# Places of routed tokens by quarters, rows scattered within the loop over groups, scaling on ScalarE

## The chip, the cores and the metric

One core of a Trainium2 chip runs the whole program. The metric is the device time of one execution in microseconds; the time before is the median of three runs.

## The reference, cut to what matters

The model has two blocks over 8192 tokens (32 sequences of 256) with 128 features. Each block computes `x + s * silu(g)`, where `s` comes from an attention branch and `g` from a feed-forward branch with experts, both fed with the normalised `x`. Block 0 has two transformer layers and 64 experts with a capacity. The change lies in block 1, whose routed part sends each token to one of 32 experts:

```python
shared_out = _swiglu(x, shared_gate_w, shared_up_w, shared_down_w)
logits = x @ gate_w
topk_ids = jnp.argmax(logits, axis=-1)
topk_val = jnp.max(logits, axis=-1)
scores = jax.nn.sigmoid(topk_val)[:, None]
xs = x * scores
tokens_per_expert = jnp.zeros((E,), jnp.int32).at[topk_ids].add(1)
order = jnp.argsort(topk_ids)
sorted_x = xs[order]
g = _grouped_mm(sorted_x, routed_gate_w, tokens_per_expert)
u = _grouped_mm(sorted_x, routed_up_w, tokens_per_expert)
d = _grouped_mm(jax.nn.silu(g) * u, routed_down_w, tokens_per_expert)
inv = jnp.argsort(order)
routed_out = d[inv]
return (shared_out + routed_out).reshape(b, s, h)
```

Its attention branch is a linear attention with 16 heads of 8 features, a product of two states per sequence, a norm over the features and an output product. Sequences don't depend on one another.

## The kernel before

The 64 tiles of 128 tokens are worked on in 16 groups of 4 tiles (`NG` = 16, `GT` = 4). Each piece of work is a Python generator that yields after a step; `run` takes a step of each of its generators in turn, and `rolling(steps, lag)` starts a new group every `lag` rounds. So the written order is an interleaving. A planner then orders each engine's queue anew, from dependencies, free buffers and its own estimates of time, and on the chip each queue runs strictly in order. NoSync edges given by hand bind that order on one engine without a wait.

Block 1 has these stages.

1. **The loop over groups** (`begun`, a `rolling` of `begin(g)` with lag 2). Its first steps lie beside the last units of block 0; `drain(begun)` runs the rest. For a group, `route(g)` loads the two parts of the block 0 experts' result (c_g, c_m, SyncE queue), adds them on GpSimd (POOL, L185), applies silu (ACT), multiplies and adds on VectorE (DVE), and normalises with `normed(..., act)`: statistics on DVE (L108, L109), small operations on POOL (L110 to L119), four activations on ACT (L121) into c_xn. Then come transposes on TensorE (PE, L131), router products (L205), maxima and indices on DVE (L213, L214), one-hot rows `hot`, the score, and the scaled rows `s_all` by four POOL operations (L224). Products with a triangle and with ones give each token's rank among those of its group with the same expert, and `before[:, g + 1]`, the counts of each expert up to this group (L232 to L240). `shared1(g)` computes the shared expert (L250 to L267).
2. **Places.** After the loop the counts of all groups are known. Each expert's share of the 96 pages (`S1` = 96 pages of 128 rows in the DRAM buffer `xslot`) is its count rounded up to 128. DVE computes where each expert's pages begin and from that `dest`, the place of each token (L811 to L839), and `widx`, the weight row of each page, with one small product on PE.
3. **Scatter beside linear attention.** `send()` issues one indirect DMA a tile from POOL's queue (L845, 64 in all; "sends" below), each of 128 rows of 129 numbers, the last being the token's number. After each send the written order has one step of `attending`, a `rolling` with lag 3 of `linear_attention(g)` for the first 15 groups. Such a group has ten steps and an end, 11 turns, and so 165 turns in all. Its norm (`normed(..., vec)`, eighth step) has three small operations on POOL (L110, L111, L113) between DVE's statistics and DVE's scaling; an order edge holds a later send behind the last norm written. The group's result goes to `s_all` (L929), the same memory that the sends read.
4. **Pages beside attention.** `routed()` takes pages in fours. It loads four pages from `xslot` (e_x, L938, after the last eight sends have landed), transposes them, and for each page loads the owner's weights (e_w, 384 KB, L958), multiplies (L961, L970) and scatters the result to `back` by an indirect DMA on POOL (L975). Four pages are five turns, 120 in all; a turn of attention and a turn of pages alternate, and what is left of the one runs alone.
5. **The end.** The sixteenth attention group runs beside `finish(g)`: load from `back`, two products with the identity that add the shared part (L996, L997), silu, multiply, add, store.

Work tiles are shared by tags ("gate", "tok", "chan", "out", "wide") in two pools, `works[0]` with one buffer a tag and `works[1]` with two; `work(n)` picks one of them by n % 3. In the loop "gate" holds c_g and "out" the shared expert's result.

Of the kernel before, what the change touches and what calls it, by code (L numbers as in the profile page):

```python
# [16 lines left out]
F32 = mybir.dt.float32  # L17
I32 = mybir.dt.int32
# [42 lines left out]
def recurrent_kernel(ctx: ExitStack, tc: tile.TileContext, x, consts, small0, wsd, wgu, wd, small1, bias1, wr, out):  # L61
# [87 lines left out]
    def room(pool_, gs):  # L149
        for g in gs:  # L150
            x_at[g] = pool_.tile([P, GT, D], F32, name=f"x_{g}")
            xt_at[g] = pool_.tile([P, GW], F32, name=f"xt_{g}")
            if g % 4 == 0:
                hots[g // 4] = pool_.tile([P, NT // 4, E1], F32, name=f"hot_{g // 4}")
# [4 lines left out]
    def begin1(pool_):  # L159
        t = at1["sw_c"] = pool_.tile([P, n_s1 - cut], F32, name="sw_c")  # L160
        sp.dma_start(t, small1[:, cut:])
        at1["rank"] = pool_.tile([P, NT], F32, name="rank")
        at1["before"] = pool_.tile([P, NG + 1, E1], F32, name="before")
        vec.memset(at1["before"][:, 0], 0.0)
        at1["ones"] = pool_.tile([P, P], F32, name="ones")
        vec.memset(at1["ones"], 1.0)
        at1["eiota"] = pool_.tile([P, E1], F32, name="eiota")
        pool.iota(at1["eiota"], [[1, E1]], base=0, channel_multiplier=0, allow_small_or_imprecise_dtypes=True)
        room(pool_, range(EARLY))
# [7 lines left out]
    def route(g):  # L177
# [20 lines left out]
        normed(wk, x_at[g], xn, act)  # L198
        yield
# [23 lines left out]
        for j in range(GT):  # L223
            pool.tensor_scalar(s_all[:, g * GT + j], xn[:, j], score[:, j : j + 1], 0.0, ALU.mult, ALU.add)  # L224
# [15 lines left out]
        vec.tensor_reduce(at1["rank"][:, tl], pos, AX.X, ALU.add)  # L240
        yield
# [53 lines left out]

    def begin(g):
        yield from route(g)
        yield from shared1(g)
# [499 lines left out]
    before, rank, ones = at1["before"], at1["rank"], at1["ones"]  # L798
# [3 lines left out]
    siota = w1p.tile([P, 1], F32, name="siota")  # L802
    pool.iota(siota, [[0, 1]], base=0, channel_multiplier=P, allow_small_or_imprecise_dtypes=True)

    drain(begun)


    dest = w1p.tile([P, NT], I32, name="dest")
    widx = w1p.tile([1, S1], I32, name="widx")
    pad = w1p.tile([P, E1], I32, name="pad")  # L810
    vec.tensor_scalar(pad, before[:, NG], float(P - 1), None, ALU.add)  # L811
    vec.tensor_scalar(pad, pad, 7, 7, ALU.logical_shift_right, ALU.logical_shift_left)
    padf = w1p.tile([P, E1], F32, name="padf")
    vec.tensor_copy(padf, pad)
    ends = w1p.tile([P, E1], F32, name="ends")
    vec.tensor_tensor_scan(ends, ones[:, :E1], padf, 0.0, ALU.mult, ALU.add)
    vec.tensor_tensor(padf, ends, padf, ALU.subtract)

    late = w1p.tile([S1, E1], F32, name="late")
    owner = w1p.tile([S1, 1], F32, name="owner")  # L820
    vec.tensor_scalar(late, ends[:S1], siota[:S1], None, ALU.is_le)
    vec.tensor_reduce(owner, late, AX.X, ALU.add)
    vec.tensor_scalar(owner, owner, float(E1 - 1), float(P), ALU.min, ALU.mult)
    diag = w1p.tile([S1, S1], F32, name="diag")
    vec.tensor_scalar(diag, ident[:S1, :S1], owner, None, ALU.mult)
    ps = bank()
    pe.matmul(ps[:1, :S1], ones[:S1, :1], diag, start=True, stop=True)
    vec.tensor_copy(widx, ps[:1, :S1])
    nq = 4
    for q in range(nq):  # L830
        tq = slice(q * NT // nq, (q + 1) * NT // nq)
        gq = slice(q * NG // nq, (q + 1) * NG // nq)
        vec.tensor_tensor(before[:, gq], before[:, gq], bcast(padf, 1, NG // nq), ALU.add)
        hq = hots[q].rearrange("p (g t) e -> p g t e", t=GT)
        for j in range(GT):
            vec.tensor_tensor(hq[:, :, j], hq[:, :, j], before[:, gq], ALU.mult)
        pos = w1p.tile([P, NT // nq], F32, name=f"pos{q}")
        vec.tensor_reduce(pos, hots[q], AX.X, ALU.add)
        vec.tensor_tensor(dest[:, tq], pos, rank[:, tq], ALU.add)  # L839

    sent, returned, last_norm = [], [], []

    def send():
        for t in range(NT):
            ins = pool.indirect_dma_start(  # L845
                out=xslot, out_offset=bass.IndirectOffsetOnAxis(ap=dest[:, t : t + 1], axis=0),
                in_=s_rows[:, t], in_offset=None,
            )

            if sent:  # L850
                tc.declare_no_dep(ins.ins, group="sent", reason="the rows are disjoint")
            tc.add_to_no_dep_group("sent", ins.ins)
            sent.append(ins)
            if last_norm:
                tc.add_manual_dep(ins.ins, last_norm[-1].ins.name, order, reason="norms go before")
            yield

    def linear_attention(g):
# [6 lines left out]
        q2 = work(g).tile([P, GT, D], F32, tag="gate", name="l_q2").rearrange("p t d -> p (t d)")  # L865
# [48 lines left out]
        o = work(g).tile([P, GT, D], F32, tag="tok", name="l_o")  # L914
# [7 lines left out]
        ot = work(g).tile([P, GW], F32, tag="chan", name="l_ot")  # L922
# [11 lines left out]
    def routed():  # L934

        for i in range(S1 // GT):
            xg = wk.tile([P, GT, D + 1], F32, name="e_x", bufs=2)
            ins = sp.dma_start(xg, rows(xslot, i))  # L938
            for d in sent[-8:]:
                tc.add_manual_dep(ins.ins, d.ins.name, waits, reason="reads what all the scatters wrote")  # L940
# [6 lines left out]
            xt = work(i).tile([P, GW], F32, tag="chan", name="e_xt")  # L947
            act.copy(xt, ps)  # L948
            ys = work(i).tile([P, GT, D], F32, tag="out", name="e_ys")
            yield  # L950
            for j in range(GT):
                wt = wk.tile([P, 3 * F1], F32, name="e_w", bufs=6)
                at = i * GT + j
                row = nc.values_load(
                    widx[:, at : at + 1], engines={mybir.EngineType.SP}, min_val=0, max_val=(E1 - 1) * P,
# [30 lines left out]
    def finish(g):  # L986

        tl = slice(g * GT, (g + 1) * GT)
        tag = ("gate", "tok", "chan", "out")[g % 4]
        gr = work(g // 4 + g).tile([P, GT, D], F32, tag=tag, name="f_g")  # L990
        ins = sp.dma_start(gr, rows(back, g))
        for d in returned[-8:]:
            tc.add_manual_dep(ins.ins, d.ins.name, waits, reason="reads what all the scatters wrote")

        ps = bank("sc", 4)
        pe.matmul(ps, ident, xt_at[g], start=True, stop=False)  # L996
        pe.matmul(ps, ident, gr.rearrange("p t d -> p (t d)"), start=False, stop=True)  # L997
        act.activation(gr, ps.rearrange("p (t d) -> p t d", d=D), AF.Silu)
        yield
        vec.tensor_tensor(gr, gr, s_all[:, tl], ALU.mult)  # L1000
        vec.tensor_tensor(gr, gr, x_at[g], ALU.add)
        sp.dma_start(rows(out, g), gr)
        yield

    sending, routing = send(), routed()
    attending = rolling([linear_attention(g) for g in range(NG - 1)], 3)
    while len(sent) < NT:
        next(sending, None)
        next(attending, None)
# [92 lines left out]
```

## Time and profile before

| | |
|---|---|
| median of 3 runs | 1380.33 us (1379.74 to 1383.29) |
| the profiled execution's own time | 1386.77 us |
| its span, from the first to the last instruction | 1384.8 us |
| mean granted TensorE clock | 0.958 |
| busy: PE, DVE, ACT, POOL | 1244.0, 956.0, 775.8, 684.9 us |
| last ranks of the loop (L240) | 959.6 us |
| first and last send (L845) | 963.7 and 1074.5 us |
| last page scatter (L975) | 1341.3 us |

The page of the profile gives busy time by engine, the span in slices, the DMA queues, the chain of work that ended last, and groups of instructions with their mean time and the idle time before them. A table by stage gives, for each stretch of time, each engine's busy time with the number of instructions in brackets, the granted clock, the share of time in which the DMA engines were busy, and GB/s. A timeline row has the start, the time taken, engine, line, operation, what is written and read, how many, and in square brackets how long the engine sat idle before it and what ended that.

### The profile page before, as it was taken

To read this page: it belongs to the slowest core of one execution; us is meant where nothing else is said; L and a number is where in the kernel's file an instruction comes from. 1 tells how busy PE (TensorE), PEld (TensorE's weight loads), DVE (VectorE), ACT (ScalarE), POOL (GpSimd) and SP (SyncE) were. 2 spreads that over 40 slices of the span, in tenths; PEclk is the share of its full clock that TensorE was granted. 3 is DMA by queue.
4 is the path that set the end of the run, shared out by engine and by line. 5 is a ranking of instruction groups with operands and counts; after the bars stand their busy time and mean duration, and the time that the engine had idled before them with its cause. 6 is when DMAs were issued, how large, how long until landed. Compare 5 with 4: busy or idle time off the path is not lost.

```text
span 1384.8 us, 22930 instructions
## 1 busy us (share of the span) xinstructions
PE 1244.0 (90%) x7425; PEld 877.7 (63%) x7425; DVE 956.0 (69%) x3091; ACT 775.8 (56%) x1842; POOL 684.9 (49%) x1052
## 2 busy tenths in 40 slices
PE   6988999899989999999997989899766889999898
PEld 4645665656655776667764666566454778788763
DVE  4689898968965566765655878777755665666437
ACT  1775566576746767667675566453533545545343
POOL 6254428272246766676646354442566344343440
PEclk9999999999989999999998999999977899999999
DMA  6021323310221221122201142512311557666667
GB/s 187 11 54 54 103 85 96 109 42 11 92 82 27 54 52 45 28 39 54 52 7 35 47 122 69 142 32 68 110 49 52 166 158 217 194 195 202 182 196 204
DMA packets 141927, 128.95 MB, mean 93 GB/s; under 512 B 17808, under 2 KB 117104, under 8 KB 141680
## 3 DMA queue, kind: packets, MB, share of 16 engines
q1 hardware_dynamic: 130032, 111.72, 27.5%
q0 software_dynamic: 11776, 15.78, 5.1%
q8 instruction: 59, 0.97, 0.3%
q14 instruction: 60, 0.49, 0.1%
HBM read 85.20 MB, written 42.25 MB: 92 GB/s over the span
## 4 chain that ended last, share of the span: by engine, by line
PE 56%; DVE 18%; ACT 8%; POOL 6%; issue 6%; DMA 4%; another core or an unknown queue 1%; SPq 0%; POOLq 0%; ACTq 0%; DVEq 0%
PE ps_mm L673 6%; PE ps_mm L655 6%; PE ps_sc L578 4%; PE ps_mm L619 3%; PE ps_tr L131 3%; PE ps_tr L610 3%; PE ps_mm L550 3%; PE ps_sc L961 3%; PE ps_sc L880 3%; PE ps_mm L970 3%; DMA e_x<-xslot 2%; PE ps_tr L902 2%; PE ps_mm L560 2%; PE ps_mm L633 2%; POOL bn_rs L111 2%
## 5 line engine op out<-in xcount | busy, mean ns | idle before, releaser
L975 POOL DMA_INDIRECT back<-e_ys,e_toi x96 | 97.0, 1011 | 139.0 <-ACT e_ys L974 112.9
L593 ACT ACTIVATE a_pr<-ps_sc,a_nm 128x256 f32<-128x256 f32 x256 | 119.2, 478 | 68.1 <-DVE a_nm L584 68.1
L110 POOL TENSOR_SCALAR bn_rs<-bn_mv 128x4 f32<-128x4 f32 x112 | 26.0, 232 | 229.2 <-DVE bn_mv L109 214.0
L655 PE MATMUL ps_mm<-xt,sw 128*128 128x512 f32 x256 | 134.3, 629 | 3.8 <-ACT r_ex L390 2.0
L124 POOL TENSOR_SCALAR z<-s_rows,bn_rs 128x128 f32<-128x128 f32 x256 | 129.4, 517 | 6.9
L673 PE MATMUL ps_mm<-sw,m_h 128*128 128x128 f32 x1024 | 127.3, 279 | 2.1 <-ACT a_at L625 1.1
L673 PEld LDWEIGHTS ps_mm<-sw,m_h 128*128 128x128 f32 x1024 | 119.6, 193 | 14.0 <-issue 5.3
L660 DVE SCALAR_TENSOR_TENSOR m_h<-m_h,m_z 128x512 f32<-128x512 f32 x128 | 89.7, 707 | 46.4 <-ACT m_h L659 45.3
L516 POOL DMA_INDIRECT moe<-e_y,sidx x64 | 93.0, 1453 | 57.8 <-ACT e_y L512 41.6
L111 POOL TENSOR_TENSOR bn_rs<-bn_rs,power 128x4 f32<-128x4 f32 x112 | 115.1, 1028 | 1.3
L657 ACT ACTIVATE m_z<-ps_mm,fold 128x512 f32<-128x512 f32 x128 | 86.8, 687 | 36.4 <-PE ps_mm L655 36.1
L584 DVE TENSOR_REDUCE a_nm<-ps_sc 128x2 f32<-128x512 f32 x128 | 83.1, 681 | 34.4 <-PE ps_sc L578 30.6
L961 PE MATMUL ps_sc<-e_xt,e_w 128*128 128x128 f32 x768 | 101.5, 279 | 3.0 <-ACT e_xt L948 2.2
L961 PEld LDWEIGHTS ps_sc<-e_xt,e_w 128*128 128x128 f32 x768 | 94.6, 195 | 10.0 <-issue 5.9
L578 PE MATMUL ps_sc<-a_qk,a_qk 64*128 64x256 f32 x512 | 96.8, 417 | 0.5 <-ACT a_pr L593 0.3
L610 PE MATMUL ps_tr<-con,a_pr 128*128 128x128 f32 x512 | 76.9, 284 | 9.8 <-ACT a_pt L611 6.0
L610 PEld LDWEIGHTS ps_tr<-con,a_pr 128*128 128x128 f32 x512 | 59.7, 146 | 40.9 <-issue 21.2
L659 ACT ACTIVATE m_h<-m_z 128x512 f32<-128x512 f32 x128 | 80.1, 635 | 1.4
L619 PE MATMUL ps_mm<-a_pt,a_v 128*64 128x256 f32 x512 | 73.3, 406 | 5.6 <-ACT e_y L512 2.8
L845 POOL DMA_INDIRECT xslot<-s_rows,dest x64 | 65.1, 1018 | 24.3 <-issue 18.5
L611 ACT COPY a_pt<-ps_tr 128x512 f32<-128x512 f32 x128 | 70.6, 590 | 10.0 <-PE ps_tr L610 8.7
L970 PE MATMUL ps_mm<-e_w,e_hs 128*128 128x128 f32 x384 | 61.7, 288 | 13.9 <-DVE e_hs L967 9.6
(234 smaller groups left out, 2985.7 us busy)
## 6 DMA issues: line engine op xcount, KB each, us to landing
e_w<-in_wr_dram SPq DMA_DIRECT2D x96, 384.0 KB
xslot<-zero SPq DMA_DIRECT2D x4, 1548.0 KB
e_x<-xslot SPq DMA_DIRECT2D x24, 258.0 KB
e_wg<-in_wgu_dram SPq DMA_DIRECT2D x16, 384.0 KB
x_in<-in_x_dram SPq DMA_DIRECT2D x16, 256.0 KB
tab<-s_rows SPq DMA_DIRECT2D x16, 256.0 KB
moe<-s_y SPq DMA_DIRECT2D x16, 256.0 KB
moe<-zero SPq DMA_DIRECT2D x4, 1024.0 KB
```

What stands on the lines that cost most here:

```text
L111: pool.tensor_tensor(rs[:, 0], rs[:, 0], power, ALU.pow)
L124: ins = pool.tensor_scalar(dst[:, j], src[:, j], rs[:, 1, j : j + 1], rs[:, 0, j : j + 1], ALU.add, ALU.mult)
L516: pool.indirect_dma_start(out=moe0[e % 2], out_offset=bass.IndirectOffsetOnAxis(ap=sidx[:, 4 * q + e : 4 * q + e + 1], axis=0), in_=ye[:, ...
L578: pe.matmul(sc[h][:, j * SEQ : (j + 1) * SEQ], qk[0][hd, q0 : q0 + P], qk[1][hd, b * SEQ : (b + 1) * SEQ], start=True, stop=True,)
L593: act.activation(pr[:, n], sc[h][:, j * SEQ : (j + 1) * SEQ], AF.Exp, bias=nm[:, n : n + 1], accum_out=su[:, n : n + 1],)
L610: pe.transpose(pts[:, n * P : (n + 1) * P], pr[:, n, k * P : (k + 1) * P], ident)
L619: pe.matmul(av[h * DPH : (h + 1) * DPH, :SEQ], v[:, 2 * b + k, h * DPH : (h + 1) * DPH], pt[:, k, h], start=k == 0, stop=k == 1,)
L655: pe.matmul(ps, par("w1", l * FF0 + f * P, P), xt, start=True, stop=True)
L673: pe.matmul(ps[:, j * D : (j + 1) * D], hs[f][:, j * P : (j + 1) * P], par("w2", l * FF0 + f * D, D), start=f == 0, stop=f == 3,)
L961: pe.matmul(ps[:, c * P : (c + 1) * P], wt[:, c * P : (c + 1) * P], xt[:, j * P : (j + 1) * P], start=True, stop=True,)
L970: pe.matmul(yp[:, :D], hs[:, c * P : (c + 1) * P], wt[:, 2 * F1 + c * D : 2 * F1 + (c + 1) * D], start=c == 0, stop=c == 1,)
L975: ins = pool.indirect_dma_start(out=back, out_offset=bass.IndirectOffsetOnAxis(ap=toi[:, j : j + 1], axis=0), in_=ys[:, j], in_offset=None,)
```

## The change

Expert places are handed out by pages, a quarter of the tokens at a time. After every fourth group, `place(q)` looks at the counts so far, rounds them up to pages, and gives each expert the pages that it newly needs behind those given out before. An expert's pages are then no longer consecutive. A token's place is its rank, plus the rows given before, plus a jump where it falls into a new page. `place(3)` also sums the owners of the pages and makes `widx`.

The sends stand within the loop: behind the norm of group g, up to four sends whose quarter was placed (group 7 and later), which gives 36 sends within the loop and 28 after it. `keep_in_program_order` holds each send behind the POOL instruction written before it. The rows are scaled by four activations on ACT instead of four operations on POOL. The page loads wait for all sends, e_w has five buffers instead of six, and attention and pages use fixed pools for their tiles. The places' tiles use the tags "out" and "gate" of `works[1]`.

```diff
         xn = wk.tile([P, GT, D], F32, tag="tok", name="c_xn")
         normed(wk, x_at[g], xn, act)
+        for _ in range(4):
+            if len(sent) < NT and g >= len(sent) // (NT // 4) * 4 + 7:
+                next(sending)
         yield
...
         for j in range(GT):
-            pool.tensor_scalar(s_all[:, g * GT + j], xn[:, j], score[:, j : j + 1], 0.0, ALU.mult, ALU.add)
+            act.activation(s_all[:, g * GT + j], xn[:, j], AF.Copy, scale=score[:, j : j + 1])
...
+    def place(q):
+        wk = works[-1]
+        full, off, ends, before = at1["full"], at1["off"], at1["ends"][:, q], at1["before"]
+        tq, gq = slice(q * NT // 4, (q + 1) * NT // 4), slice(q * NG // 4, (q + 1) * NG // 4)
+        pad = wk.tile([P, E1], I32, name="p_pad")
+        vec.tensor_scalar(pad, before[:, (q + 1) * NG // 4], float(P - 1), None, ALU.add)
+        vec.tensor_scalar(pad, pad, 7, 7, ALU.logical_shift_right, ALU.logical_shift_left)
+        vec.tensor_copy(full[:, q + 1], pad)
+        new = wk.tile([P, E1], F32, name="p_new")
+        vec.tensor_tensor(new, full[:, q + 1], full[:, q], ALU.subtract)
+        last = at1["ends"][:, q - 1, E1 - 1 : E1] if q else 0.0
+        vec.tensor_tensor_scan(ends, at1["ones"][:, :E1], new, last, ALU.mult, ALU.add)
+        w = wk.tile([P, GT, NG // 4, E1], F32, tag="out", name="p_w")
+        jump = wk.tile([P, E1], F32, name="p_jump")
+        vec.tensor_tensor(jump, ends, full[:, q + 1], ALU.subtract)
+        vec.tensor_tensor(jump, jump, off[:, q], ALU.subtract)
+        vec.tensor_tensor(w[:, 0], bcast(full[:, q], 1, NG // 4), before[:, gq], ALU.subtract)
+        vec.tensor_tensor(w[:, 1], bcast(off[:, q], 1, NG // 4), before[:, gq], ALU.add)
+        vec.tensor_copy(w[:, 2], bcast(jump, 1, NG // 4))
+        vec.scalar_tensor_tensor(new, new, 0.0, jump, ALU.is_gt, ALU.mult)
+        vec.tensor_tensor(off[:, q + 1], off[:, q], new, ALU.add)
+        yield
+        hq = hots[q].rearrange("p (g t) e -> p g t e", t=GT)
+        got = wk.tile([P, 3, NT // 4], F32, name="p_got")
+        for n in range(3):
+            sel = wk.tile([P, NT // 4, E1], F32, tag="gate", name="p_sel")
+            vec.tensor_tensor(sel.rearrange("p (g t) e -> p g t e", t=GT), hq, bcast(w[:, n], 2, GT), ALU.mult)
+            vec.tensor_reduce(got[:, n], sel, AX.X, ALU.add)
+            yield
+        rank = at1["rank"][:, tq]
+        vec.tensor_tensor(got[:, 0], rank, got[:, 0], ALU.is_ge)
+        vec.tensor_tensor(got[:, 0], got[:, 0], got[:, 2], ALU.mult)
+        vec.tensor_tensor(got[:, 1], got[:, 1], rank, ALU.add)
+        vec.tensor_tensor(at1["dest"][:, tq], got[:, 0], got[:, 1], ALU.add)
+        placed.add(q)
+        yield
...
     def begin(g):
         yield from route(g)
+        if g % 4 == 3:
+            yield from place(g // 4)
         yield from shared1(g)
...
     def send():
         for t in range(NT):
...
             sent.append(ins)
-            if last_norm:
-                tc.add_manual_dep(ins.ins, last_norm[-1].ins.name, order, reason="norms go before")
+            tc.keep_in_program_order(ins)
             yield
...
-            for d in sent[-8:]:
+            for d in sent:
...
-                wt = wk.tile([P, 3 * F1], F32, name="e_w", bufs=6)
+                wt = wk.tile([P, 3 * F1], F32, name="e_w", bufs=5)
...
-        q2 = work(g).tile([P, GT, D], F32, tag="gate", name="l_q2").rearrange("p t d -> p (t d)")
+        q2 = works[0].tile([P, GT, D], F32, tag="gate", name="l_q2").rearrange("p t d -> p (t d)")
```

The old block of places after the loop (L808 to L839) is gone. Likewise the tiles of attention l_o and l_ot lie in `works[1]` and `works[0]`, and those of the pages e_xt and e_ys in `works[1]`. The page results' loads in `finish` wait for all scatters instead of the last eight. The written order after the loop is as it was: a send and a step of attention in turn until all 64 sends are written, then pages beside attention.

## Prediction

> **What bounds the kernel now.** I read the page first (PE busy 90% of the span, POOL 49%), then a table by stage of the part that the change touches: loop over groups to 963 us, rows scattered 963 to 1076, first page of the experts at 1090, pages beside attention to 1298, pages alone to 1342, end.
>
> ```profile
> core 0: us, PE busy (x) PEld busy (x) DVE busy (x) ACT busy (x) POOL busy (x), PEclk, DMA share, GB/s
> 963.00:1013.00 50.00, 35.61 (x138) 20.60 (x137) 35.85 (x102) 22.37 (x25) 31.20 (x34) 0.86 0.35 110
> 1013.00:1076.00 63.00, 44.98 (x192) 33.49 (x192) 37.59 (x99) 24.16 (x26) 41.08 (x46) 0.76 0.16 51
> 1090.00:1298.00 208.00, 191.19 (x1386) 165.39 (x1385) 126.76 (x371) 106.00 (x225) 87.47 (x99) 0.98 0.66 196
> 845.00:963.00 118.00, 109.77 (x608) 78.68 (x607) 87.18 (x407) 52.84 (x115) 41.41 (x89) 0.97 0.24 67
> ```
>
> While rows are scattered no engine is full: PE is busy 81 of 113 us, at a clock of 0.76 to 0.86. In the loop before it and among the pages after it PE is busy 92 to 93%. So the scatter stage is the loose one. POOL's timeline tells why.
>
> ```profile
> 979.00 0.96 POOL L845 DMA_INDIRECT xslot<-s_rows,dest  x1 [0.30 <-issue]
> 980.27 0.97 POOL L845 DMA_INDIRECT xslot<-s_rows,dest  x1 [0.30 <-issue]
> 991.02 0.19 POOL L110 TENSOR_SCALAR bn_rs<-bn_mv 128x4 f32<-128x4 f32 x1 [9.79 <-DVE bn_mv L109]
> 992.77 1.05 POOL L845 DMA_INDIRECT xslot<-s_rows,dest  x1 [0.17 <-issue]
> ...
> 1006.53 0.20 POOL L110 TENSOR_SCALAR bn_rs<-bn_mv 128x4 f32<-128x4 f32 x1
> ...
> 1012.36 0.98 POOL L845 DMA_INDIRECT xslot<-s_rows,dest  x1 [0.30 <-issue]
> ...
> 1074.47 0.95 POOL L845 DMA_INDIRECT xslot<-s_rows,dest  x1 [0.30 <-issue]
> ```
>
> Sends follow one another every 1.27 us (979.00, 980.27), but each stretch of 11 to 13 ends in an attention group's norm, for which POOL waits: five such waits, 27 us in the list of waits. So 64 sends tied to five norms last 963.7 to 1075.4, where 64 x 1.27 would be 81. The 28th send starts at 1012.36, after the second norm. Until the last has landed no page can start; the chain of waits shows it:
>
> ```profile
> 1074.47 2.36 DMA xslot<-s_rows,dest
> 1076.98 2.97 DMA e_x<-xslot
> ```
>
> What a page and an attention group cost beside each other comes from two counts by stage: page scatters (L975), then stores of finished attention groups (L929).
>
> ```profile
> 1102.00:1298.00 196.00, 69.42 (x69) 0.98 0.65 193
> 1311.00:1342.00 31.00, 16.02 (x18) 1.00 0.64 203
> ...
> 1102.00:1298.00 196.00, 5.49 (x9) 0.98 0.65 193
> ```
>
> Pages alone: 18 starts, 17 intervals, from 1310.1 to 1341.3, 1.84 us each. The nine stores run from 1102.4 to 1298.0, eight intervals: 24.5 us a group, in which the written order has 8.8 pages (11 attention steps, 5 page steps to 4 pages). Those pages alone would take 16.2, so beside pages **a group costs 8.3 us more**. Its PE time there (busy by count for L862, L870, L880, L902, L913, L131, L927) is 11.0. In the scatter stage groups came at 997.1, 1021.5, 1036.6, 1055.9 and 1074.1: **19.3 us each**.
>
> **The change, part by part.**
>
> *Sends in the loop.* Four at each of the groups 7 to 14 and 15 make 36; 28 stay behind the loop, one to an attention step. The 13th and 24th attention step hold the first two norms, and sends stay behind norms as before. Of the 28, the first 12 need places of the third quarter only and may go before the loop ends; the rest need the last quarter's places, some 7 us after its ranks, and the two norms. Those norms came at 991 and 1006.5, so the last send starts near 1012.4 instead of 1074.5: **-62.1 us**, with landing and first page after it unchanged (the last send started 15.2 us before the first page's scatter at 1089.7).
>
> *Attention that this leaves for later.* 64 steps lay beside the sends, 28 do now; 36 steps (3.3 groups) move. Of 165 steps 137 remain against 120 page steps, where 101 remained. So 19 steps move to where pages ran alone: 19/11 x 8.3 = **+14.3**. The other 17 have no pages beside them and come with the end stage, whose last group and 16 final products keep PE busy 35.8 of 43 us. I take PE time, 17/11 x 11.0 = **+17.0**, as the final products can fill gaps; ends 12.8 (8.3 a group) and 30 (19.3).
>
> *Places by quarters on DVE.* By rows of this trace a `place` is: pad .173 + .172, cast .182, scan .225, six 128x32 operations at .19, three 128x128 at .277 (L833), three times a 128x512 product at .695 (L194) with its sum at .667 (L838), four 128x16 at .156, three for the owner at .55: 7.8 us, 7.2 of it before the places are there. Three lie in the loop, 23.4; the fourth (8.6 with its diagonal) replaces 10.8 after it. From 840 to 963 DVE is busy 91.4 of 123 us; 23.4 more is 93%, and PE is at 93% too. With 31.6 idle the cost lies between 0 and 23.4. DVE's queue is in order: behind a place stand the maxima and one-hot rows that PE's rank products wait for, and a place can itself wait, as its work tiles use the slots of c_g and f_y.
>
> *Sends on POOL in the loop.* The scaling takes 19.9 us off POOL (48 instructions, 845 to 963); 36 sends at 1.27 bring 45.7, so 67 of 118 us. Each quarter's first send waits for DVE's places; behind it stand the next group's sum (L185) and norm (L110 to L119), for which ACT's c_xn and then PE wait. The last norm is done at 919.2, its c_xn runs at 935.9: 17 us of cover. Gone, three waits of 7.2 us would cost up to 22. I take **+10** for DVE and POOL together, nearer to the idle time; ends 0 and 45.
>
> The sends here run beside a DVE that is busy 65% and take 954 / 958 / 2108 ns (least, median, most), so I keep 1.27 us. [...]
>
> *Scaling on ScalarE.* Four 128x128 activations take 1.65 us (L121), 26 us in all; ACT is busy 57 of 123 us and this is hidden. Without that cover it is 1.65 us a group. It ends ACT's waits for POOL's read of c_xn (10.8 us, six times), but PE hardly waited on those: nothing.
>
> *At nothing:* e_w with five slots instead of six (the list of waits has no wait for e_w between 1075 and 1345; cover is five pages at 2.8 us, and if it failed perhaps 5 us); waiting for all sends instead of the last eight (one queue, the last lands last); pages in another order (96 pages and as many weight loads); fixed slots for attention and pages.
>
> **Sum:** -62.1 + 14.3 + 17.0 + 10 = -20.8 us. The profiled execution took 1386.8 us, 2 more than its span of 1384.8, and 6.4 more than the median of 1380.3. So about 1366 for a profiled execution and **1360** for the median.
>
> **Rivals.**
>
> 1. *The loop grows by more than it saves (slower).* Place: the loop from group 7 on, where DVE and POOL are given 23 and 26 us net, and POOL stands at a send until DVE has the places. Price up to 45; from 31 on nothing is gained, and 41 gives 1390. For it: DVE at 83% from 880 to 900, PE at 96% in the last 43 us. Against: 31.6 us idle on DVE, POOL 40 us ahead of PE.
> 2. *The unpaired attention is paid at the scatter stage's price.* 17 steps at 19.3 a group are 30 instead of 17, with 15 in the loop: -3 to -8, so 1372 to 1377. For it: a lone group is a chain over five engines. Against: 16 final products are there to fill it.
> 3. *The moved attention is nearly free.* All 36 steps at 8.3 a group, 27, and a loop that doesn't grow: -35, 1345.
> 4. *The rows don't leave early.* If sends end up behind the norms of later groups, all 64 stay late, and the added DVE work is paid: 1385 to 1400.
>
> **How the numbers follow.** Main course 0.55, rival 1 0.18, rival 2 0.12, rival 3 0.10, rival 4 0.05. A difference within 0.3% (4 us) can't be told from none here. Faster: 0.52 + 0.08 + 0.10 = 0.70; same: 0.02 + 0.02 + 0.04 + 0.02 = 0.10; slower: 0.01 + 0.16 + 0.03 = 0.20. The main course alone is 1349 to 1375 (17 steps from 15 to 20, loop from 2 to 22). The range reaches over rivals 2 and 3 and half of rival 1: 1342 to 1390.
>
> **What would show it.** Right: 36 sends before the loop's last ranks, 28 after or around its end; about 50 us from the loop's end to the last send with two norms among them; first page scatter near 1038; mixed pages still near 2.8 us; attention stores after the last page scatter, and an end stage near 58 us instead of 43. Wrong: last ranks later than about 990 (rival 1); POOL waiting on dest for long before a send with PE idle; mixed pages above 3.0 us; an end stage over 75 us (rival 2).

## The result, and the profile after

The changed kernel took 1398.85 us (median of 4 runs, 1397.09 to 1400.21), the kernel before beside it 1381.81 us (4 runs): a ratio of 1.0133, with a 95% interval of 1.0103 to 1.0163. The forecast was 1360, faster. The profiled execution took 1397.09 us over a span of 1395.3.

By stages, in us (before, after, difference; predicted difference):

| stage | before | after | difference | predicted |
|---|---|---|---|---|
| last ranks of the loop | 959.6 | 999.2 | +39.6 | +10 |
| from there to the last send | 114.9 | 54.0 | -60.9 | -62.1 |
| from there to the first page scatter | 15.2 | 13.9 | -1.3 | 0 |
| page scatters, first to last | 251.7 | 267.7 | +16.0 | +14.3 |
| end | 43.5 | 60.5 | +17.0 | +17.0 |

All terms but one came out within 2 us. The loop's did not: it grew by more than is saved, which is what rival 1 forecast. ("Last ranks" is L253 in the changed kernel; a send is L371, a sum of c_g and c_m L195.) The table by stage of the changed kernel, whose stretches are the loop, the sends behind it, the pages and the end:

```profile
core 0: us, PE busy (x) PEld busy (x) DVE busy (x) ACT busy (x) POOL busy (x), PEclk, DMA share, GB/s
845.00:999.00 154.00, 106.84 (x512) 74.49 (x511) 89.91 (x433) 57.79 (x144) 73.84 (x93) 0.84 0.26 76
999.00:1053.00 54.00, 40.26 (x179) 24.86 (x177) 37.62 (x106) 25.34 (x31) 17.28 (x21) 0.91 0.30 89
1067.00:1335.00 268.00, 249.46 (x1790) 213.40 (x1790) 164.89 (x480) 140.01 (x296) 113.93 (x129) 0.99 0.61 188
1335.00:1395.00 60.00, 48.63 (x186) 25.96 (x184) 46.00 (x103) 23.35 (x31) 5.34 (x10) 0.98 0.53 150
```

In the loop PE is busy about as long as before (109.8 us then, 106.8 now) in 30% more time, and no engine is full: PE 69%, DVE 58%, POOL 48%. So the loop didn't get an engine that is busy all the time; it got waits. Its list of waits, 845 to 1003:

```profile
POOL c_g L195 <- DMA c_g<-moe: 33.0, 2, 20.7
ACT c_xn L121 <- POOL bn_rs L119: 31.6, 6, 12.5
...
POOL bn_rs L110 <- DVE bn_mv L109: 24.9, 4, 12.2
PE ps_tr L131 <- ACT c_xn L121: 22.2, 7, 7.8
...
DVE before L250 <- remote: 10.7, 1, 10.7
```

PE waits for c_xn, ACT for the norm on POOL, and POOL for DVE's statistics. (Before, ACT waited for L119 only 5.8 us between 860 and 964.) "Remote" stands where the profile knows no instruction that ended the wait. POOL's timeline shows what stands around a norm:

```profile
915.01 0.98 POOL L371 DMA_INDIRECT xslot<-s_rows,dest  x1 [3.45 <-ACT c_g L203]
916.82 0.96 POOL L371 DMA_INDIRECT xslot<-s_rows,dest  x1 [0.82 <-issue]
...
919.35 0.96 POOL L371 DMA_INDIRECT xslot<-s_rows,dest  x1 [0.30 <-issue]
920.39 0.19 POOL L110 TENSOR_SCALAR bn_rs<-bn_mv 128x4 f32<-128x4 f32 x1
920.66 0.22 POOL L117 TENSOR_SCALAR bn_rs<-bn_mv 128x4 f32<-128x4 f32 x1
921.03 1.02 POOL L371 DMA_INDIRECT xslot<-s_rows,dest  x1 [0.15 <-issue]
922.07 1.18 POOL L111 TENSOR_TENSOR bn_rs<-bn_rs,power 128x4 f32<-128x4 f32 x1
923.45 1.04 POOL L371 DMA_INDIRECT xslot<-s_rows,dest  x1 [0.20 <-issue]
924.52 0.21 POOL L119 TENSOR_TENSOR bn_rs<-bn_rs 128x4 f32<-128x4 f32 x1
```

Four sends stand ahead of the norm and two between its four operations. The plainest case is earlier: from 854.0 to 867.0 seven sends and a norm with two more sends in it pass through POOL, and from 861.5 on PE, DVE and ACT are idle together, for 5.5 us; they start again when the norm ends (ACT has waited 12.5 us for L119 then). From group 10 on the norms come at 907.6, 924.5, 935, 942, 947 and 966 us; before they came at 895, 898, 904, 908, 916 and 919.

### The profile page after: what moved, and what is told of

It reads as the page before. It is cut to its first block, busy times and chain, and to the rows that moved or that the text cites. A ratio compares the mean times of both kernels' runs of the same rounds, so it can differ in the third digit from the quotient of the medians.

```text
span 1395.3 us, 22978 instructions
## 1 busy us (share of the span) xinstructions
PE 1239.2 (89%) x7425; PEld 872.4 (63%) x7425; DVE 969.0 (69%) x3159; ACT 795.1 (57%) x1906; POOL 657.6 (47%) x988
## 5 line engine op out<-in xcount | busy, mean ns | idle before, releaser
L751 DVE SCALAR_TENSOR_TENSOR m_h<-m_h,m_z 128x512 f32<-128x512 f32 x128 | 89.7, 706 | 43.1 <-ACT m_h L750 42.3
L996 PEld LDWEIGHTS ps_sc<-e_xt,e_w 128*128 128x128 f32 x768 | 95.6, 195 | 14.4 <-issue 8.3
L371 POOL DMA_INDIRECT xslot<-s_rows,dest x64 | 63.8, 997 | 43.5 <-issue 36.5
L1009 ACT COPY e_ys<-ps_mm 128x128 f32<-128x128 f32 x96 | 25.4, 265 | 87.4 <-PE ps_mm L1005 78.2
## 6 DMA issues: line engine op xcount, KB each, us to landing
e_x<-xslot SPq DMA_DIRECT2D x24, 258.0 KB
```

Source lines behind the costliest of these rows:

```text
L751: vec.scalar_tensor_tensor(h, h, 1.0, z, ALU.add, ALU.mult)
L996: pe.matmul(ps[:, c * P : (c + 1) * P], wt[:, c * P : (c + 1) * P], xt[:, j * P : (j + 1) * P], start=True, stop=True,)
```

## The experiments

Kernels with the same chip in the table ran beside the kernel before on it. Chip I gave the result above; whether it is one of the later ones isn't known. Ratios are of medians, while the stages come from one profiled execution of each kernel. For most kernels that execution lies within 5 us of the median; those of e8 (1369.8 us, median 1362.3) and e10 (1390.9, median 1383.5) lie 7 us above, the slowest of theirs.

| kernel | chip (before there) | ratio, 95% interval | last ranks | last send, later by | pages | end |
|---|---|---|---|---|---|---|
| before | I (1381.8) | 1 | 959.6 | 114.9 | 251.7 | 43.5 |
| changed | I | 1.0133 [1.0103, 1.0163] | 999.2 | 54.0 | 267.7 | 60.5 |
| e1 sends written after the loop | II (1371.7) | 1.0112 [1.0073, 1.0151] | 988.8 | 89.2 | 243.3 | 43.2 |
| e2 sends two groups later | II | 1.0147 [1.0086, 1.0208] | 993.1 | 61.5 | 267.9 | 50.3 |
| e4 before, scaling on ACT | II | 0.9943 [0.9912, 0.9975] | 952.3 | 104.2 | 248.5 | 43.1 |
| e5 changed, scaling on POOL | II | 1.0040 [1.0015, 1.0065] | 989.2 | 45.0 | 261.5 | 61.8 |
| e8 norms before sends | II | 0.9934 [0.9909, 0.9959] | 986.9 | 45.7 | 260.7 | 60.8 |
| e10 own slots | II | 1.0081 [1.0054, 1.0108] | 1006.4 | 44.5 | 262.4 | 61.9 |
| e9 own slots, norms first | II | 0.9912 [0.9885, 0.9939] | 973.8 | 44.4 | 261.7 | 61.9 |
| e7 own slots, sends after loop | II | 1.0154 [1.0117, 1.0191] | 962.8 | 120.4 | 243.5 | 43.0 |
| e11 e9, statistics before places | III (1370.4) | 0.9875 [0.9821, 0.9929] | 973.5 | 44.8 | 266.1 | 52.3 |
| e13 e9, scaling on POOL | III | 0.9952 [0.9927, 0.9976] | 980.2 | 45.1 | 261.3 | 61.0 |
| e14 shared slots, sends after loop | III | 1.0124 [1.0055, 1.0193] | 963.8 | 113.5 | 246.4 | 43.1 |
| e12 e9, attention in the tail | IV (1371.6) | 1.0010 [0.9981, 1.0038] | 987.3 | 66.4 | 258.0 | 43.3 |
| e15 changed | V (1369.6) | 1.0018 [0.9998, 1.0037] | 986.8 | 46.0 | 259.0 | 61.9 |
| e16 before | V | 1.0012 [0.9993, 1.0031] | 960.8 | 105.8 | 245.1 | 43.5 |
| e17 e4 with filler | V | 1.0009 [0.9994, 1.0025] | 956.2 | 108.2 | 243.7 | 43.0 |
| e18 e9, two sends a step | V | 1.0027 [0.9999, 1.0055] | 963.9 | 73.1 | 269.0 | 43.1 |
| e19 changed | VI (1382.9) | 1.0116 [1.0078, 1.0154] | 1004.9 | 54.9 | 265.8 | 60.6 |
| e20 norms before sends (as e8) | VI | 1.0082 [1.0054, 1.0110] | 999.0 | 54.8 | 265.8 | 61.8 |

### First: which part of the change

e1 and e2 change the condition in `route`, e4 and e5 one line each:

```diff
 e1  -        for _ in range(4):
     +        for _ in range(0):
 e2  -            if len(sent) < NT and g >= len(sent) // (NT // 4) * 4 + 7:
     +            if len(sent) < NT and g >= len(sent) // (NT // 4) * 4 + 9:
 e4, in the kernel before:
     -            pool.tensor_scalar(s_all[:, g * GT + j], xn[:, j], score[:, j : j + 1], 0.0, ALU.mult, ALU.add)
     +            act.activation(s_all[:, g * GT + j], xn[:, j], AF.Copy, scale=score[:, j : j + 1])
 e5, in the changed kernel: the same line the other way
```

> The places stay in the loop and the scaling on ScalarE; only the 36 sends are taken out of the loop, so all 64 follow it, one to an attention step. Theory A (sends in POOL's queue hold up the norms of the loop's groups): the last ranks come back from 999 us to 960 to 970, the sends take about 111 us again, and the time is near the kernel before, 1380 to 1392. Theory B (the places' work on VectorE and their tiles in the slots of the loop stretch it): the last ranks stay near 990 to 1000 and the time is 1410 to 1425. Theory C (the scaling in ScalarE's queue stretches it): as B.

> As the changed kernel, but the first sends of a quarter stand behind the norm of the sixth group after its last (g >= 9, 13) instead of the fourth; 28 sends lie in the loop and 36 behind it. Theory A1 (POOL stands at sends whose places are not there yet): the waits before the 17th and 33rd send are gone, the last ranks come at 965 to 980, and the time is 1370 to 1385. Theory A2 (the sends' own 1.27 us between one norm and the next cost the time): last ranks 985 to 1000, time 1390 to 1402. Theory B (places) and C (scaling): last ranks near 999, time 1398 to 1406, as eight more sends follow the loop.

> The kernel before with one edit: the rows are scaled by four ScalarE activations a group instead of four POOL operations. Theory C (the scaling in ScalarE's queue stretches the loop): last ranks 970 to 1000 instead of 959.6, time 1390 to 1420. Theories A and B: last ranks within 5 us of 959.6 and the time within 5 us of the kernel before.

> The changed kernel with the scaling back on POOL, four operations of about 0.4 us a group. Theory C: the last ranks come earlier than 999 us, at 960 to 985, and the time falls to 1360 to 1385. Theory A: POOL has 1.5 us more a group in a queue that already holds up the loop, so last ranks 999 to 1015 and time 1398 to 1412. Theory B: no difference beyond 5 us.

e1 and e2 didn't do what they were made for. The planner moves a send to where its place is ready, wherever it was written: 44 and 47 sends still went before the last ranks (48 in the changed kernel), the first of them at 847.9 and 852.8 us. They tell nothing on the sends. e4 settles the scaling in the kernel before, and theory C fell: on ScalarE the last ranks come at 952.3, against 959.6 and 960.8 in the two profiles of the kernel before, and the median falls by 8.2 us. POOL is free of 44 operations, between 860 and 960 us alone, that stood among sums and norms. e5's time (1377 us) lies in theory C's range and its last ranks (989.2) in none; beside the changed kernel on chip V (e15, below) they are 2.4 us later, so there the scaling's place shows little.

### Second: sends, slots and places apart

To hold the sends, e7, e8 and e9 tie each by an order edge to a POOL operation of a norm (e7: that of the last group, with `range(0)` as in e1). e7, e9 and e10 give places tiles of their own.

```diff
+            scaled.append(pool.tensor_tensor(rs[:, 1], rs[:, 1], rs[:, 0], ALU.mult))
...
+            tc.add_manual_dep(ins.ins, scaled[-1].ins.name, order, reason="norms go before")
             tc.keep_in_program_order(ins)
... own slots:
-        w = wk.tile([P, GT, NG // 4, E1], F32, tag="out", name="p_w")
+        w = wk.tile([P, 2, NG // 4, E1], F32, name="p_w", bufs=1)
...
-            sel = wk.tile([P, NT // 4, E1], F32, tag="gate", name="p_sel")
...
+            for h in range(2):
+                sel = wk.tile([P, NT // 8, E1], F32, name="p_sel", bufs=1)
```

> The changed kernel, with every send ordered on GpSimd behind the norm that is written before it (the four of a step behind that group's own norm). The slots of the tiles of places stay those of the gate loads. Theory Q (sends stand in front of norms in GpSimd's queue, and that is the loop's growth): the last rank falls from 999.2 to about 965-970 us, the program to 0.985-0.99 of the kernel before. Theory S (the tiles of places take the slots that the gate loads of the last groups need, so the planner runs group 14 after group 15 and its load lands late): the last rank stays at 990-1000 and the ratio at 1.005-1.015. Theory D (VectorE's time for places in the loop): likewise 990 or more.

> The changed kernel, with tiles of their own for the places (the 2 KB tile of weights cut to its two parts that differ by group, the selection made in two halves of 1 KB, one buffer each), so that no gate load waits for a step of places; the sends are free to float as in the changed kernel. Theory S: groups run in order again, the last rank falls to about 965-970 us and the program to 0.985-0.99 of the kernel before. Theory Q: the sends still stand in front of norms, last rank 985-1000, ratio 1.005-1.015. Theory D: 990 or more, for VectorE's work is the same or slightly more (6 instructions more a quarter).

> Both edits together: tiles of their own for the places, and every send behind the norm written before it. Theories Q and S: last rank about 955-965 us, the last send 45-60 us later, ratio 0.975-0.985, whichever of the two is the cause (each alone then tells which). Theory D: the same work on VectorE, last rank still 985 or more and the ratio 1.00 or more.

> Tiles of their own for the places, and all 64 sends ordered behind the last group's norm: the places stay in the loop, no send does. Theory Q: last rank 950-960 us as with the scaling alone (952.3), the last send about 85-100 us later, ratio 0.99-1.00. Theory S: the same. Theory D: last rank 980 or more, since the places alone make the growth; ratio 1.01 or more.

Theory D fell as a whole: with places in the loop and every send behind its last norm (e7; 11 sends still start before the last ranks) the last ranks come at 962.8, 10.5 us after e4's. Places have a price, and it is the +10 that was meant for places and sends together. e9 adds the sends, norms first: 973.8, another 11.0, and 9 us later than either theory expected. e8 is e9 with shared slots: 986.9, another 13.1 by the profiles; but e8's is its slowest execution, and by the medians, on the same chip, it is 3.3 us (1362.3 against 1359.0, intervals that overlap). So how much the slots cost by themselves stays open. e10 lets the sends float with own slots: 1006.4, 32.6 more than e9 by the profiles, 24.5 by the medians. There a sum that ACT's silu waits for stands behind fourteen sends and two norms in POOL's queue, and ACT, DVE and PE are idle together from 864.7 to 878.2. Its list of waits, 862 to 880:

```profile
DVE c_g L204 <- ACT c_g L203: 14.6, 1, 14.6
ACT c_g L203 <- POOL c_g L195: 13.8, 1, 13.8
```

So neither Q nor S alone is right: with own slots the order of the sends matters (e10 against e9), and with norms first four sends a step still cost 11.0 (e9 against e7). e7 also shows what a queue of sends does to attention: 59 sends in a row stand before an attention group's norm, as its waits from 990 to 1032 tell, and its last send comes 120.4 us after the ranks.

```profile
DVE l_o L117 <- POOL bn_rs L115: 32.2, 1, 32.2
```

### Third: statistics, slots without sends, and attention earlier

```diff
 e11 (on e9): places written one step later, sends from `+ 8`, and on three kinds of place operation
     +    tc.add_manual_dep(ins.ins, aggr[-1].ins.name, order, reason="statistics go before")
 e13 (on e9): the scaling's line back on POOL
 e14 (changed kernel, `range(0)`): each send ordered behind the norms of all groups
     +            for n in scaled:
     +                tc.add_manual_dep(ins.ins, n.ins.name, order, reason="norms go before")
 e12 (on e9):
     -        if n >= 999:
     +        if n >= 82:
                  next(attending, None)
```

> The kernel with own slots and norms first (1358.99 us, ratio 0.9912, last rank 973.8), with each quarter's places written one step later and its first instructions and products ordered on VectorE behind the norm statistics written before them; sends begin one group later (44 in the loop's list, as many after it as before less 4). In the kernel with own slots and norms first the fourth aggregate of group 15's statistics came at 948.9 us, 8 us after its third, behind the places of quarter 2. Theory P (part of the places' price of some 10 us is that order, and not VectorE's time): last rank 962-968, ratio 0.983-0.988. Theory D (it is VectorE's time): last rank 972-978, ratio 0.990-0.995.

> The kernel with own slots and norms first, with the scaling of the rows back on GpSimd: 4 instructions of 0.44 us for each of the last groups, 16 groups. The scaling alone on ScalarE made the kernel before 8 us faster in its last rank, yet taking it back in the changed kernel made that one faster too. Theory G (GpSimd is the engine that is short in the loop once the sends are there): last rank 980-990, ratio 1.00. Theory N (the scaling's place matters only by the order that the planner then finds): last rank within 5 us of 973.8, ratio 0.989-0.995.

> The changed kernel with its shared slots, and every send ordered behind the norms of all 16 groups: places in the loop in the gate loads' slots, no send in it. With own slots the same order gave a last rank of 962.8. Theory S (the shared slots cost the loop some 13 us whatever the sends do): last rank 974-980, the last send 90-120 us later, ratio 1.015-1.03. Rival: the slots cost only when sends fill GpSimd's queue: last rank 960-966, ratio 1.005-1.017.

> The kernel with own slots and norms first (ratio 0.9912, last rank 973.8, first attention store at 1012, end stage 61.9 us), with one attention step written after each of the last 24 steps of the loop, 24 of 165 steps. After the loop of that kernel PE is busy 23.5 of the 30 us from 1000 to 1030 and the end stage holds the attention steps that no page is beside. If those steps are paid at PE's time (1.0 us a step, the price that the prediction used for the unpaired ones) and the loop's tail has no room for them, the loop grows by as much as the end stage shrinks: ratio 0.988-0.994. If they fill PE's idle time before 1030, the attention stores come some 8-10 us earlier and the end stage falls to 45-55: ratio 0.983-0.987. If they delay the last groups' norms and ranks as the sends did: last rank 985 or later, ratio 0.995 or more.

e11 leaves the last ranks where they were (973.5 and 973.8), so theory P fell by them. Its ratio is the lowest of all and lies in theory P's range, but its interval takes in e9's. e13's last ranks (980.2) lie at the edge of theory G, its ratio (0.9952) just above theory N: by the last ranks the scaling is worth 6 us there. e14 is the telling one. It has the changed kernel's slots and no send ahead of a norm (16 stand between the last norm and the last ranks), and its last ranks come at 963.8, 1.0 us after e7's and 23 before those of the changed kernel on chip V. So shared slots cost the loop next to nothing without sends ahead of its norms. What they do shows in SyncE's queue: the last c_g load goes out at 909.7 us in e7 and 916.4 in e9, but at 933.6 in e14 and 958.0 in e8. There the planner puts group 14 behind group 15, and on the chip that load stands right behind a store of f_y. e12 went the third way: attention steps among the last groups delay their ranks by 13.5 us and the last send by 22 more, for 18.6 us gained at the end.

### Fourth: size, and the chip

```diff
 e17 (on e4, five slots for e_w), for the groups 3, 7 and 11:
     +        scr = works[-1].tile([P, 256], F32, name="scr", bufs=1)
     +        vec.memset(scr, 1.0)
...
     +        for n in range(4):
     +            for _ in range(4):
     +                vec.tensor_tensor(scr, scr, scr, ALU.max)
     +            yield
     +        vec.tensor_tensor(scr, scr, scr, ALU.max)
     +        vec.tensor_tensor(scr, scr, scr, ALU.max)
 e18 (on e9):
     -        for _ in range(4):
     +        for _ in range(2):
```

> The changed kernel itself, unaltered, on the chip of the experiments. Its first profile shows PE, VectorE and ScalarE all idle from 980 to 989 us while GpSimd sends, and matmul records are missing there; the variants with the same order of sends have no such stretch and last ranks of 988.8 to 993.1. If that stretch belongs to the kernel, the last rank comes at 995-1002 again and the ratio to the kernel before is 1.012-1.017. If it belongs to that one execution, the last rank comes at 985-993 and the ratio lies lower, 1.005-1.012.

> The kernel before, unaltered, on the chip of the experiments, for its stages: last rank 950-960 (959.6 in its first profile, at a time that was 0.7% longer), the last send 105-115 later, pages 248-252, end 43.

> The kernel before with the scaling on ScalarE (last rank 952.3, ratio 0.9943), and in the places of the first three quarters' steps 18 VectorE products of 128x256 on a tile of their own with a memset, some 7.4 us a quarter: as much VectorE time as a place takes, tied to nothing else; five slots for e_w, and the places after the loop as in the kernel before. Places in the loop with no send among them made the last rank 962.8. If their price is VectorE's time, the last rank comes at 960-965 and the ratio at 1.000-1.004. If it is their order and their waits, 952-956 and 0.993-0.998.

> The kernel with own slots and norms first (last rank 973.8, last send 44.4 later, ratio 0.9912; without sends in the loop its last rank was 962.8), with two sends at a step in place of four: 18 before the end of the loop's list, 46 after. If the sends' price in the loop goes by their number, the last rank comes at 967-970 and the last send 65-75 later, ratio 0.995-1.005. If it is only what stands in front of a norm at a time, the last rank comes at 962-966.

> The changed kernel once more, on one chip with the kernel whose norms go ahead of the sends (shared slots in both). Their profiles on two chips agree in every stage (last rank 986.8 and 986.9, spans 1367.7 and 1368.0), their medians don't (1372.0 and 1362.3, ratios 1.0018 and 0.9934). If the order of sends against norms costs anything with these slots, this kernel's ratio lies 0.5-0.9% above that of the other; if the medians differed by the chip alone, within 0.3%.

> The changed kernel with every send ordered behind the norm written before it, on one chip with the changed kernel. If the order costs anything with shared slots, its ratio is 0.5-0.9% lower than that of the changed kernel; if not, within 0.3% of it, and the last ranks of the two profiles within 3 us of each other.

e18: 27 sends before the last ranks cost 1.1 us (963.9 against e7's 962.8, on two chips), 41 in fours 11.0. The price does not go by the number; that it goes by how many stand with one norm is what fits. e17 is split: by last ranks (956.2 against 952.3) VectorE's time is 3.9 of the places' 10.5, by the ratio it is more; the two kernels ran on two chips, and this stays open. e20 lies 0.34% under e19, with intervals that overlap, and the last ranks differ by 5.9 us: on chip VI, with shared slots, the order of sends against norms is worth some 5 or 6 us, not the loop's growth. Across chips II and V the same two kernels lie further apart (0.9934 for e8, 1.0018 for e15), but that holds the chips' difference too.

e15 was the surprise. On chip V the changed kernel takes the time of the kernel before (1.0018, 0.9998 to 1.0037); on chips I and VI it is 1.2 to 1.3% slower. The kernel of e8 goes the same way, from 0.9934 on chip II to 1.0082 on chip VI (e20). Up to 978 us the two executions agree within 1 us. Then come these 12 us, first on chip I, then on chip V:

```profile
978.00:990.00 12.00, 2.67 (x22) 2.51 (x21) 0.80 (x4) 0.00 (x0) 7.89 (x9) 0.72 0.16 51
```

```profile
978.00:990.00 12.00, 11.13 (x63) 7.49 (x62) 8.55 (x43) 5.32 (x14) 8.43 (x9) 1.00 0.25 78
```

POOL sends in both. On chip I PE, DVE and ACT stand idle; DVE waits for PE's product L249 (the "remote" line above) and starts 10.2 us after the profile's modelled end of it.

## Why the prediction was wrong

**The failed step: "I take +10 for DVE and POOL together".** It was +39.6 on chip I (959.6 to 999.2), and +26.0 on chip V (960.8 to 986.8), where the profiles of both kernels are free of stops like the one near 980. Of the 13.6 between the two, that stop is 8.8. With 39.6 in place of 10 and the other terms as measured, the sum gives the 1397 of the profiled execution.

The runs take the +26.0 apart by one change after another, so that the parts must add up to it: scaling -8.5 (e4), places +10.5 (e7 against e4), sends in fours with norms ahead +11.0 (e9 against e7), and +13.0 for shared slots and free order together (e15 against e9). Each is a difference of two profiles, some on two chips, and good to some us; how the 13.0 divides is open, as e8 shows. Taken in one step, with the slots as they are, sends are worth 23.0 (e15 against e14).

Rival 1 had the sign and nearly the size (up to 45), but one of its reasons didn't show: POOL hardly stood at a send for DVE's places. Before the first send of each of the three quarters in the loop it was idle for 0.8, 3.5 and 0.7 us.

**Why sends cost some 23 and not next to nothing.** The prediction took POOL's load over the whole loop, "67 of 118 us", and 17 us of cover. But the sends stand only with the last groups, and there the load is per group. An estimate from the rows: a norm of four operations, 1.84 us before (0.25 + 0.32 + 1.01 + 0.27), a sum of 1.27, four sends of 1.27: 8.2 us. Ranks of groups 9 to 15 came every 7.4 us before (915.1 to 959.6), and every 8.3 in e7 with its places (913.0 to 962.8). So in those groups POOL was asked for all of a group's time or more, and what came late was hard to make good. e8's timeline shows a group with no wait left in it; e14's, with the same slots, has waits for DVE's statistics before the norms there:

```profile
923.49 0.20 POOL L121 TENSOR_TENSOR bn_rs<-bn_rs 128x4 f32<-128x4 f32 x1
923.85 1.05 POOL L373 DMA_INDIRECT xslot<-s_rows,dest  x1 [0.16 <-issue]
...
928.27 0.97 POOL L373 DMA_INDIRECT xslot<-s_rows,dest  x1 [0.30 <-issue]
929.31 0.19 POOL L112 TENSOR_SCALAR bn_rs<-bn_mv 128x4 f32<-128x4 f32 x1
...
930.85 0.45 POOL L121 TENSOR_TENSOR bn_rs<-bn_rs 128x4 f32<-128x4 f32 x1
```

```profile
907.19 0.21 POOL L112 TENSOR_SCALAR bn_rs<-bn_mv 128x4 f32<-128x4 f32 x1 [4.88 <-DVE bn_mv L111]
...
910.93 0.54 POOL L112 TENSOR_SCALAR bn_rs<-bn_mv 128x4 f32<-128x4 f32 x1 [2.01 <-DVE bn_mv L111]
...
917.80 0.47 POOL L112 TENSOR_SCALAR bn_rs<-bn_mv 128x4 f32<-128x4 f32 x1 [4.81 <-DVE bn_mv L111]
```

Norms end in e8 at 908.7, 923.7, 931.3, 939.6, 946.8 and 968.4 us. In e14 a norm that comes nearly as late (898.8, 20.6 us after the one before it; 23.3 in e8) is followed by 908.9, 913.0, 919.8, 924.3 and 943.9. So the four norms after the late one take 38.1 us in e8 and 25.5 in e14: 12.6 of the 23.1 us between their last ranks. Ten more were lost before 908.7, in steps. POOL isn't without waits in e8: 13.9 us for statistics before 906.9, and 14.4 for group 14's load before 961.2. With two sends a group needs 5.7 us, under 7.4, and e18's loop is e7's.

A slower PE goes along with it. The granted clock was 0.97 in the loop before, 0.94 in e14's, 0.88 in e15's and 0.84 in the changed kernel's on chip I, and the same product of 128x512 (L250 in the kernel before) took 604, 619, 658 and 704 ns in them on average. How much of the growth is that, and whether the waits bring it about, isn't separated here.

**"28 stay behind the loop".** They didn't: 48 sends, not 36, went before the last ranks, the first at 848.4. `keep_in_program_order` binds a send to the instruction written before it, and the planner took the sends as early as their places allowed. That -60.9 came so near the forecast all the same is because the last quarter's places (1009.5 us) and two attention norms set the end: the last two sends stand behind norms at 1041.6 and 1051.5, as the prediction had it, and the count before them mattered little. By e20 the sends' place ahead of norms is some 6 us of the loop's growth on chip VI, not all of it.

**Right.** The sends' gain (-60.9, and -59.8 on chip V); the moved attention, +16.0 and +13.9 on chip V; the unpaired steps, +17.0 and +18.4. The 17.0 is in part luck: it was reckoned as PE's time, but PE is busy only 12.9 us longer in the end stage (35.8 us before, 48.6 now). e7 and e14 confirm the last two from the other side: with the sends behind the loop both stages are as before (243.5 and 246.4, 43.0 and 43.1). e_w with five slots cost nothing there either. Keeping 1.27 us a send was right: the 64 sends took 955 / 962 / 1507 ns (least, median, most) with DVE busy 58% of the loop. The longest took 1.51 us here, 2.11 in the kernel before and 2.15 in e16, and what lengthened those few isn't shown. Of a place's price: the listed rows add up to 8.0 us and not 7.8, as the code has five small operations and not six; that changes nothing.

**Scaling: "nothing".** It was a gain of 7 to 8.5 us in the kernel before and 6 in e13 against e9, though only 2.4 in e5 against e15; the prediction had only looked at ACT's waits and not at what POOL's 44 operations held up.

**The shared slots.** The sentence "a place can itself wait, as its work tiles use the slots of c_g and f_y" named the right slots, but what was late was a load. POOL waited 33.0 us for two c_g loads (20.7 and 12.3), and each of them left SyncE's queue 0.5 us behind a store of f_y, with no wait of its own (the row holds four stores, the last at 955.8):

```profile
917.99 38.19 SPq L338 DMA_DIRECT2D moe<-f_y  x4
956.27 0.46 SPq L192 DMA_DIRECT2D c_g<-moe  x1
```

That the planner chose this order because a place holds the slot is inferred from the kernels with own slots, where the last load goes out 24 and 42 us earlier (e7 against e14, e9 against e8).

The versions that beat the kernel before are e9 (0.9912, 0.9885 to 0.9939), e11, e8, e13 and e4; e4, the scaling alone, has 0.9943 (0.9912 to 0.9975). That the places and sends bring anything beyond the scaling is not shown. On chips I and VI e9 was not run, and e8's gain was gone there.

## What to carry to other kernels

Work that is moved into a loop is to be set against the time of one turn of that loop, on the engine whose queue it enters, in the turns that get it: 57% over the whole loop was, by estimate, all of a group's time in its last groups (8.2 us against 7.4 to 8.3). Two sends a turn cost 1 us here, four cost 11. Where a planner orders the queues, read the order that it made before costing an edit: it moved sends ahead of norms and, where slots were shared, turned two groups round. And a stage read from one execution is to be held against the medians: e8's loop looked 13 us longer than e9's, their medians lie 3 us apart.

## What was not expected of the hardware

On chips I and VI, which may be one chip, PE stops beside long streams of sends. In the changed kernel's streams of 17 and 14 sends PE, DVE and ACT go idle together 11 to 15 us after the stream begins and start again within 3 us of its end: for 8.8 and 6.3 us on chip I (from 980.1 and 1021.1), 9.1 and 6.2 on chip VI (986.7 and 1026.8); in e20 there 13.2 and 6.3. On chips II, III and V the streams of 17 and 20 sends of e15 and e8, and of 30 and 34 in e9 and e11, have no such stop. (In e7, e14 and e18 the three engines also idle together, for 31.3, 23.5 and 13.5 us; in e7 that is the attention norm behind the sends, by its list of waits.) From chip V to chip I the changed kernel loses 27 us of its median, 15 of them in these two stops, and the kernel before, whose streams have at most 13 sends, 12 us, 9.1 of them in its scatter stage. So the size of the slowdown, 1.3% or nothing, goes with the chip. The granted clock is 0.72 in the 12 us shown above, but PE has only 22 products in them, against 63 on chip V. Part of PE's signals is missing in the profile of chip I (1599 are in its trace and 1674 in that of chip V, for the same kernel). What stops PE there stays open, and so does whether the missing signals have to do with it.

The measurement's own noise can be read from e16: the kernel before against itself gave 1.0012 (0.9993 to 1.0031).
